# Cross-attention on the ring of eight PSUM banks, in text order on four engines, begun inside the self-attention's last steps, with routing behind its last tile

## The chip, the cores and the metric

One core of a Trainium2 chip runs the whole program in one launch. The metric is the device time of one execution in microseconds (us). The core has five engines with a queue of instructions each: PE (TensorE, matmuls and transposes through PE), DVE (VectorE), ACT (ScalarE), POOL (GpSimd) and SP, which here only issues DMAs. Each engine takes its instructions strictly in the order of its queue, and semaphores make one wait for another. PSUM has eight banks of 128 x 512 floats; PE writes there, and DVE or ACT copy from there to SBUF.

## The reference

A decoder layer on x of shape (2, 1024, 256), that is 2048 tokens in 16 tiles of 128, in fp32, cut to what matters here:

```python
x = x + attn(layernorm(x), ...)             # 16 heads, softmax + relative bias, then its own norm
x = x + xattn(layernorm(x), ctx, ctx, mask) # 16 heads of 16 against 77 context tokens
x = x + ffn(layernorm(x), ...)              # top-2 of 8 experts, plus a shared layer, then a norm

def xattn(query, key, value, mask, Wq, Wk, Wv, Wu, bu):
    scores = where(mask == 0, -1e9, q @ k.T)          # (b, h, 1024, 77)
    return softmax(scores) @ v  ->  heads side by side  @ Wu + bu

def ffn(x, ...):
    probs = softmax(flat @ gate_W)
    topk_w, topk_idx = top_k(probs, 2)                 # two experts per token
    out = 0.5 * gelu(flat @ shared_W + shared_b)
    for e in range(8):
        out += combine[:, e] * (gelu(flat @ W1[e] + b1[e]) @ W2[e] + b2[e])
    return norm(out)
```

## The kernel before, in words

**Self-attention (to about 549 us).** Two streams run over 128 steps of 8 per (batch, head group, half): stream A multiplies scores and takes row maxima on DVE (`mx`, L516); ten steps later (`LAG`) stream B multiplies shifted scores, ACT takes the exponent (`pt`, L560), PE multiplies by the values into one bank (`av`, L569), ACT copies that out (`part`, L581) and POOL adds it up (`avs`, L582). Once per eight steps `shift_queries` and `collect` run; every second half of the last head group, `collect` also normalizes and adds 512 tokens (a chunk c of four tiles) to the residual `xs` (`affine_residual`). Here all four engines run in the order of the text (`manual_schedule`), and every PSUM tile comes from one ring of eight banks, `one()`. Jobs that belong elsewhere are put into the table `between`, by step.

**Cross-attention and gate (549 to about 770 us).** Here only PE runs in text order; a scheduler orders DVE, ACT and POOL. PSUM is split into three tiles of two banks (`big`) and two of one. For each chunk `queries(c)` normalizes 512 tokens (statistics, `rstd` through a POOL pow L142, `xn` on DVE L163), transposes them, and projects. Then for each tile i of 128 tokens:

- scores: PE `sC` (L868), DVE adds the mask in two instructions of 616 (L875), DVE takes row maxima `cm` (L882), POOL subtracts (L883);
- ACT takes the exponent (L886);
- DVE sums rows `cs` (L888) and takes the reciprocal (L889), POOL multiplies (L890);
- `turn(i)`: 16 transposes on PE (`ppT`, L901), two copies on ACT (L902).

Per chunk `attend(c)` multiplies by the values (`pco`, L915) and by Wu (`pu`, L929) and adds to `xs` (L937); `gate(c)` normalizes again, writes `xn` to DRAM (`xnd`), and multiplies by the gate weights (`pg`, L949).

**Routing.** `choose(c)` finds the two best experts of each token in thirteen small DVE instructions (L741 to L759), `place(c)` counts the tokens ahead and builds one-hot rows and columns (L799, scaled on ACT, L807), `invert(c)` multiplies them into `places` (L817, L823). All three run chunk by chunk between the tiles. After chunk 3, a chain of small DVE instructions finds which expert owns each block of 256 slots and makes `to_row` and `from_row` (L1050, L1051): the addresses by which tokens are gathered. `shared(c)` multiplies by the shared layer's weights.

**Experts (to about 1100 us) and end.** 19 blocks of 256 slots: gather tokens (POOL's indirect DMA, L1107), transpose, two layers with Gelu between, scatter. While the first blocks are fetched, POOL takes a pow for the weights (L1075), adds a bias to `acc` and another to `xs` (eight instructions, L1187 and L190), and DVE finishes the weights (L1076 to L1078). Then results are loaded back, weighted, normalized and written.

## Time and profile before

| | us |
|---|---|
| median of 6 runs (1147.15 to 1152.01) | 1148.68 |
| profiled execution, its own time | 1149.66 |
| its span | 1147.9 |
| PE busy | 952.0 |
| DVE busy | 644.4 |
| ACT busy | 513.5 |
| POOL busy | 395.8 |

| stage of the profiled execution | from | to |
|---|---|---|
| self-attention's last `part` copy ends | | 548.85 |
| first / last POOL subtract of a tile (L883) starts | 583.00 | 715.09 |
| POOL multiply of the last tile (L890) ends | | 725.13 |
| logits of the last chunk (L741) | 765.01 | |
| `from_row` (L1051) | 781.25 | 781.44 |
| experts' first matmul (L1131) | 810.02 | |

The page gives busy time per engine, then 40 slices of the span in which a digit is tenths of busy time; PEclk is the clock granted to PE in tenths of full speed. In timelines a line has its start, its duration, engine, line of the kernel, operation, output<-inputs with shapes, and in brackets the idle time of that engine before it and what ended it. Instructions in a row of the same kind are merged (x8); a duration then runs from the first start to the last end. fp32 matmuls stand twice in the count.

### The profile page before, as it was taken

The numbers are of one execution on the slowest core, as the hardware profiler recorded it, in microseconds if no ns is written. First come the engines' busy times: TensorE is split into PE (matmuls) and PEld (weight loads), VectorE is DVE, ScalarE is ACT, GpSimd is POOL, SyncE is SP. The second block draws the span as 40 slices with busy tenths as digits, with TensorE's granted clock in tenths as the row PEclk, the third lists the DMA queues.
The fourth block names the chain that finished last, engine by engine and source line by source line (L and its number), as shares of the span: only waits on it lengthen the run. The fifth ranks groups of instructions, "written<-read, shape, count | busy, mean of one in ns | idle before, by whom it ended". The sixth has DMA issues, their size and how long they took to land. (4 is left out here: it accounts for less than half of the span.)

```text
span 1147.9 us, 15494 instructions
## 1 busy us (share of the span) xinstructions
PE 952.0 (83%) x5846; PEld 544.2 (47%) x5846; DVE 644.4 (56%) x1181; ACT 513.5 (45%) x969; POOL 395.8 (34%) x318
## 2 busy tenths in 40 slices
PE   4789999999797999999367786992799999999910
PEld 2443333333332333332134555671688888887810
DVE  5677558777876788884886688655300000000047
ACT  1328568677664678879034333321422222222201
POOL 2123223543322333334565535107323222222125
PEclk9989999999988999999689888776899999999965
DMA  8100000000000000000000000007255555554152
GB/s 166 32 1 1 1 2 1 1 1 1 1 1 1 1 2 1 1 1 1 15 0 2 18 1 19 19 19 252 64 188 194 188 176 167 175 179 158 46 165 73
DMA packets 59603, 67.07 MB, mean 58 GB/s; under 512 B 17947, under 2 KB 52408, under 8 KB 59520
## 3 DMA queue, kind: packets, MB, share of 16 engines
q1 hardware_dynamic: 44400, 53.10, 14.4%
q0 software_dynamic: 3648, 9.18, 2.3%
q10 hardware_dynamic: 11472, 3.70, 1.5%
q8 instruction: 49, 0.80, 0.3%
q14 instruction: 34, 0.28, 0.1%
HBM read 57.58 MB, written 9.18 MB: 58 GB/s over the span
## 5 line engine op out<-in xcount | busy, mean ns | idle before, releaser
L516 DVE TENSOR_REDUCE mx<-sA 128x1 f32<-128x512 f32 x512 | 317.7, 683 | 89.9 <-PE sB L552 74.9
L560 ACT ACTIVATE pt<-sB 128x512 f32<-128x512 f32 x512 | 266.3, 609 | 113.8 <-PE sB L552 113.2
L509 PE MATMUL sA<-kT,qc 32*128 32x512 f32 x1024 | 266.6, 637 | 0.0
L552 PE MATMUL sB<-qB,kT 32*128 32x512 f32 x1024 | 253.9, 626 | 10.4 <-DVE mx L516 10.4
L582 POOL TENSOR_TENSOR avs<-avs,part 128x512 f32<-128x512 f32 x112 | 143.0, 1276 | 306.2 <-ACT part L581 305.8
L1138 ACT ACTIVATE hT<-ph,b1s 128x256 f32<-128x256 f32 x152 | 72.0, 475 | 193.9 <-PE ph L1131 192.6
L1131 PE MATMUL ph<-xgT,w 128*128 128x256 f32 x608 | 138.5, 386 | 16.9 <-DVE xgT L1125 16.9
L1156 DVE TENSOR_TENSOR y<-po,b 128x512 f32<-128x512 f32 x19 | 13.1, 692 | 240.6 <-PE po L1149 240.6
L509 PEld LDWEIGHTS sA<-kT,qc 32*128 32x128 f32 x1024 | 102.7, 188 | 90.7 <-ACT pt L560 56.2
L1149 PE MATMUL po<-w,hT 128*128 128x256 f32 x608 | 138.8, 382 | 6.2 <-DVE y L1156 5.6
L569 PE MATMUL av<-pt,vaug 128*32 128x512 f32 x1024 | 141.1, 612 | 0.9 <-ACT pt L560 0.9
L1131 PEld LDWEIGHTS ph<-xgT,w 128*128 128x128 f32 x608 | 107.9, 192 | 44.6 <-DVE xgT L1125 17.7
L1149 PEld LDWEIGHTS po<-w,hT 128*128 128x128 f32 x608 | 114.2, 190 | 24.9 <-DVE y L1156 9.3
L552 PEld LDWEIGHTS sB<-qB,kT 32*128 32x128 f32 x1024 | 100.3, 187 | 51.6 <-issue 32.3
L1159 POOL DMA_INDIRECT pairs<-y,to_row x38 | 38.3, 1009 | 136.1 <-DMA pairs<-y,to_row 94.8
L1107 POOL DMA_INDIRECT xg<-xnd,from_row x38 | 37.2, 978 | 109.0 <-PE px L1121 76.6
L581 ACT COPY part<-av 128x512 f32<-128x512 f32 x112 | 68.8, 614 | 8.6 <-PE av L569 8.6
L569 PEld LDWEIGHTS av<-pt,vaug 128*32 128x32 f32 x1024 | 21.6, 109 | 101.8 <-DVE mx L516 84.6
L142 POOL TENSOR_TENSOR rstd<-rstd,nhalf 128x4 f32<-128x4 f32 x20 | 21.7, 1083 | 98.8 <-DVE rstd L141 98.4
L883 POOL TENSOR_TENSOR st<-st,cm 128x1232 f32<-128x1232 f32 x16 | 36.1, 2254 | 47.9 <-DVE cs L889 20.7
L901 PE MATMUL ppT<-ident,st 128*77 128x128 f32 x256 | 38.5, 311 | 15.3 <-POOL st L890 13.9
L902 ACT COPY PT<-ppT 77x1024 f32<-77x1024 f32 x32 | 31.2, 1007 | 36.0 <-PE ppT L901 36.0
(198 smaller groups left out, 989.2 us busy)
## 6 DMA issues: line engine op xcount, KB each, us to landing
w<-in_L_ffn_W_dram SPq DMA_DIRECT2D x38, 1024.0 KB, 5.9
b<-in_L_ffn_b_dram SPq DMA_DIRECT2D x19, 128.0 KB, 6.3
xs<-in_x_dram SPq DMA_DIRECT2D x4, 512.0 KB
xnd<-xn SPq DMA_DIRECT2D x4, 512.0 KB
w<-pairs ACTq DMA_DIRECT2D x4, 512.0 KB, 5.9
w<-pairs SPq DMA_DIRECT2D x4, 512.0 KB
out_dram<-acc SPq DMA_DIRECT2D x4, 512.0 KB, 2.8
mk<-in_mask_BxSxS_ik_dram SPq DMA_DIRECT2D x1, 616.0 KB
```

The costliest lines, as they stand in the source:

```text
L509: nc.tensor.matmul(s, lhsT=units[h // 4, "q"][r0 : r0 + 32, q0 : q0 + P], rhs=units[h // 4, "k", g % 2][r0 : r0 + 32, 512 * kh : 512 * kh ...
L516: nc.vector.tensor_reduce(largest[h][:, qt, hh : hh + 1, kh], s, AX.X, ALU.max)
L552: nc.tensor.matmul(s, lhsT=units[h // 4, "k", g % 2][r0 : r0 + 32, kt * P : (kt + 1) * P], rhs=shifted[h][r0 : r0 + 32, :], start=True, st ...
L560: nc.scalar.activation(powers[m, hh], s, AF.Exp, scale=1.0 / 16.0)
L569: nc.tensor.matmul(av[32 * hh : 32 * hh + 32, :], lhsT=vaug[:, kt, 4 * g + hh, :, b], rhs=powers.pop((m, hh)), start=True, stop=True,)
L581: nc.scalar.copy(part, av)
L582: nc.gpsimd.tensor_tensor(sums[h], sums[h], part, ALU.add)
L901: nc.tensor.transpose(pp[:T2, h, :], st[:, 8 * G + h, :], ident)
L1131: nc.tensor.matmul(ph[:, j, :], lhsT=w1[:, kc, hc * P : (hc + 1) * P], rhs=xgT[:, kc, :], start=(kc == 0), stop=(kc == 1),)
L1138: hidden[i] = nc.scalar.activation(hT[:, hc, :], ph[:, j, :], AF.Gelu, bias=b1s[:, i, hc : hc + 1])
L1149: nc.tensor.matmul(po[:, s, :], lhsT=hT[:, hc, s * P : (s + 1) * P], rhs=w2[:, hc, :], start=(hc == 0), stop=(hc == NH - 1),)
L1159: nc.gpsimd.indirect_dma_start(out=pairs[:, :], out_offset=bass.IndirectOffsetOnAxis(ap=to_row[:, k : k + 1], axis=0), in_=y[:, s, :], in_ ...
```

## The change

The diff does the following.

- **Banks.** The cross-attention, the gate and the routing use the same ring of eight single banks as the streams; the split into `big` and single tiles comes only behind routing. The mask is added in four DVE instructions of 308 per tile, `turn` copies four times 4 heads, a projection is two halves (`query(c, G)`), `shared(c)` two halves.
- **Order.** `manual_schedule` for four engines now reaches to the end of routing, so DVE, ACT and POOL also run in text order there.
- **Work moved between engines.** `xn` is made by ACT (`scale`, four activations with scale and offset); the offsets are a small DVE instruction (`offsets`). The one-hot rows are made and scaled in one DVE instruction each (`one_hots`), and ACT's scaling goes. Which engine copies a bank out is written at each call (`by_dve`, `by_act`).
- **Begun earlier.** `ask(0, 82)` and `ask(1, 103)` put statistics, scaling, transposes and projection of chunks 0 and 1 into steps 82 to 123 of the streams. `behind_step` puts the scores of tiles 0, 1 and 2 and the scaling of chunk 2 behind steps 129 to 138. In the last ten steps every third `part` copy goes to DVE.
- **Loop.** `front(i)`, `turn(i - 2)`, the jobs in `beside`, `mid(i - 1)` and `soft(i)` follow each other for tiles 3 to 16. The constants of routing (iotas) are made on POOL one per tile.
- **Routing.** `choose`, `count`, `place`, `one_hots` and `invert` run only behind the last tile, for tiles 0 to 7 together, then 8 to 11, then 12 to 15. The running count `earlier` is one reduction (`sum_up`) and further matmuls instead of one addition per tile.
- **Memory.** One SBUF tile `scrap` holds, one after another, the bias table, the weights and queries of the streams, the queries and scores of the cross-attention, and `acc`. `fsw` and `b1` are loaded by SP's queue instead of ACT's.

The core of the diff (lines that begin with a space are there before and after):

```diff
+    def offsets(c, live=None):
+        mv, r = moments.pop(c)[1], tokens[c]
         if live is not None:
             nc.vector.tensor_tensor(r[:, :4], r[:, :4], live, ALU.mult)
+        off = small.tile([P, 4], F32, tag="off", name=f"off{c}")
+        nc.vector.scalar_tensor_tensor(off, mv[:, :, 0], -1.0, r[:, :4], ALU.mult, ALU.mult)
+        tokens[c] = r, off, work.tile([P, 4, D], F32, tag="xn", name="xn")
+    def scale(c, ts=range(4)):
+        r, off, xn = tokens[c]
+        for t in ts:
+            nc.scalar.activation(
+                xn[:, t, :], xs[:, 4 * c + t, :], AF.Identity,
+                bias=off[:, t : t + 1], scale=r[:, t : t + 1],
+            )
...
-        nc.scalar.copy(part, av)
+        (by_act if m + LAG < steps + 2 or m % 3 else by_dve)(part, av)
...
+    def front(i):
+        c, t = i // 4, i % 4
+        b, st = c // 2, sts[i % 4]
+        off = mb[:, i, :].unsqueeze(1).to_broadcast([P, 4, T2])
+        for G in range(2):
+            for f in range(2):
+                s = one("sC")[:, : 4 * T2]
+                nc.tensor.matmul(s, ...)
+                h0 = 8 * G + 4 * f
+                nc.vector.tensor_tensor(
+                    st[:, h0 : h0 + 4, :], s.rearrange("p (j t) -> p j t", t=T2), off, ALU.add
+                )
+        cm = small.tile([P, H], F32, tag="cm", name="cm")
+        nc.vector.tensor_reduce(cm, st, AX.X, ALU.max)
+        nc.gpsimd.tensor_tensor(st, st, cm.unsqueeze(2).to_broadcast([P, H, T2]), ALU.subtract)
+    def soft(i):
+        nc.scalar.activation(sts[i % 4], sts[i % 4], AF.Exp)
+    def mid(i):
+        st = sts[i % 4]
+        cs = small.tile([P, H], F32, tag="cs", name="cs")
+        nc.vector.tensor_reduce(cs, st, AX.X, ALU.add)
+        nc.vector.reciprocal(cs, cs)
+        nc.gpsimd.tensor_tensor(st, st, cs.unsqueeze(2).to_broadcast([P, H, T2]), ALU.mult)
...
+    def ask(c, n):
+        jobs = {
+            0: lambda: measure(c, [0]),
+            1: lambda: measure(c, [1]),
+            4: lambda: measure(c, [2]),
+            5: lambda: measure(c, [3]),
+            8: lambda: deviation(c),
+            9: lambda: offsets(c, alive(c)),
+            10: lambda: scale(c, [0, 1]),
+            12: lambda: scale(c, [2, 3]),
+            14: lambda: turned(c, 0, by_act),
+            16: lambda: (turned(c, 1, by_dve), add_rows(c, bu)),
+            18: lambda: query(c, 0, by_act),
+            20: lambda: query(c, 1, by_dve),
+        }
+        for k, job in jobs.items():
+            between.setdefault(n + k, []).append(job)
+    ask(0, 82)
+    ask(1, 103)
+    behind_step = {
+        129: [lambda: front(0)],
+        131: [lambda: soft(0)],
+        132: [lambda: mid(0), lambda: front(1)],
+        134: [lambda: soft(1), lambda: measure(2), lambda: deviation(2)],
+        135: [lambda: mid(1), lambda: offsets(2, alive(2))],
+        138: [lambda: front(2), lambda: scale(2), lambda: soft(2)],
+    }
+    for n in range(steps + LAG + 1):
...
+        for job in behind_step.get(n, []):
+            job()
+    turned(2, 0, by_act)
+    turned(2, 1, by_act)
+    add_rows(2, bu)
+    collect(len(halves) - 1)
+    mid(2)
...
+    beside = {
+        3: [lambda: measure(3), lambda: deviation(3)],
+        4: [lambda: offsets(3, alive(3)), lambda: scale(3), lambda: query(2, 0, by_dve)],
+        5: [lambda: query(2, 1, by_dve), lambda: turned(3, 0, by_act),
+            lambda: turned(3, 1, by_dve), lambda: add_rows(3, bu)],
+        8: [lambda: query(3, 0, by_dve), lambda: query(3, 1, by_act)],
+        12: [lambda: shared(0)],
+    }
+    for c in range(3):
+        i = 4 * c + 6
+        ... attend(c, 0), attend(c, 1) at i; output(c, 0), output(c, 1) at i + 1
+        if c < 2:
+            ... measure(c), deviation(c) at i + 2
+            ... offsets(c), scale(c), keep_tokens(c), turned(c, 0, by_act),
+            ... turned(c, 1, by_dve), gate(c) at i + 3
+    turn(0)
+    for i in range(3, NT + 1):
+        if i < NT:
+            front(i)
+        turn(i - 2)
+        for job in beside.get(i, []):
+            job()
+        if i > 3:
+            mid(i - 1)
+        if i < NT:
+            soft(i)
+        if i > 5 and constants:
+            constants.pop(0)()
...
+    A, Z, C = (0, 8), (8, 12), (12, 16)
+    measure(2); deviation(2); shared(1); offsets(2); scale(2); keep_tokens(2)
+    choose(*A); turn(NT - 1); turned(2, 0, by_act); turned(2, 1, by_act); gate(2)
+    attend(3, 0); attend(3, 1); prk = count(*A); part = place(*A, prk)
+    hot0 = one_hots(0, 0, part)
+    output(3, 0); measure(3, (0, 1)); output(3, 1); measure(3, (2, 3)); deviation(3)
+    hot1 = one_hots(1, 4, part)
+    offsets(3); scale(3); keep_tokens(3); shared(2); invert(0, hot0); choose(*Z)
+    turned(3, 0, by_act); turned(3, 1, by_dve); gate(3)
+    sum_up(Z[0]); invert(1, hot1); prk = count(*Z); part = place(*Z, prk)
+    choose(*C); sum_up(C[0]); prk = count(*C); ...
+    hot2 = one_hots(2, 0, part); part = place(*C, prk); invert(2, hot2)
+    hot3 = one_hots(3, 0, part); invert(3, hot3)
```

The last block stands one call to a line in the file. `sts` has four score buffers, three in `scrap` and a fourth for tile 3, 7, 11 and 15; tile i uses `sts[i % 4]`.

## The prediction, made before the result was known

> **What bounds it now.** I read the page first, then the busy time by stage, then the timeline of the cross-attention stage engine by engine. The profiled execution took 1149.66 us (span 1147.9 and 1.8 around it), 0.98 above the median of 1148.68; I work out a difference and put it on the median.

> ```profile
> span 1147.9 us, 15494 instructions
> ...
> PE   4789999999797999999367786992799999999910
> DVE  5677558777876788884886688655300000000047
> ...
> PEclk9989999999988999999689888776899999999965
> ```

> Slices of 28.7 us. From slice 19 (550 us) to 27 no engine is near full and the TensorE clock falls to 6 to 8 tenths.

> ```profile
> core 0: us, PE busy (x) PEld busy (x) DVE busy (x) ACT busy (x) POOL busy (x), PEclk, DMA share, GB/s
> 82.00:540.00 458.00, 436.02 (x3359) 161.38 (x3362) 334.08 (x574) 326.43 (x640) 158.08 (x128) 0.98 0.00 1
> 575.00:600.00 25.00, 15.62 (x73) 9.73 (x74) 22.10 (x27) 8.17 (x8) 16.88 (x8) 0.86 0.00 0
> ...
> 680.00:720.00 40.00, 29.31 (x178) 22.20 (x180) 33.69 (x58) 16.79 (x22) 16.68 (x8) 0.84 0.04 14
> 720.00:750.00 30.00, 28.68 (x153) 18.75 (x146) 18.89 (x51) 8.52 (x16) 4.29 (x2) 0.73 0.06 19
> 750.00:770.00 20.00, 18.90 (x84) 16.25 (x84) 8.40 (x34) 4.80 (x11) 1.01 (x1) 0.76 0.08 26
> ...
> 782.00:810.00 28.00, 2.25 (x7) 1.15 (x7) 19.41 (x4) 0.00 (x0) 26.39 (x14) 0.50 0.65 228
> ```

> In the streams (82 to 540) PE is busy 95% at clock 0.98: it sets the pace. From 575 to 720, in the cross-attention's tiles, PE is at 62 to 78%, DVE at 78% (113.4 of 145) and POOL at 53% (77.3 of 145): none is full, and what counts is who waits for whom.

> ```profile
> 709.08 0.19 DVE L750 TENSOR_TENSOR cand<-cand,rank 128x32 f32<-128x32 f32 x1
> 715.21 2.17 DVE L750 TENSOR_TENSOR cand<-cand,rank 128x32 f32<-128x32 f32 x1
> 715.09 2.25 POOL L883 TENSOR_TENSOR st<-st,cm 128x1232 f32<-128x1232 f32 x1
> ...
> 713.00 1.92 PE L915 MATMUL pco<-PT,vx 77*32 77x512 f32 x16
> 718.11 0.41 PE L769 MATMUL prk<-taken,before 128*128 128x32 f32 x2 [3.18 <-DVE taken L759]
> 719.05 3.40 PE L915 MATMUL pco<-PT,vx 77*32 77x512 f32 x16
> ```

> Two things. The same DVE instruction (L750, two SBUF inputs) takes 0.19 us alone and 2.17 us while a POOL multiply of 2.25 us runs: it ends as that one ends. And a PE gap of 3.18 us is followed by sixteen `pco` matmuls in 3.40 us, which took 1.92 just before: half clock.

> ```profile
> 781.25 0.19 DVE L1051 TENSOR_SCALAR from_row<-to_row 128x46 int32<-128x46 int32 x1
> 790.48 18.38 DVE L1076 TENSOR_SCALAR wts<-wts 128x16 f32<-128x16 f32 x1 [8.96 <-POOL wts L1075]
> 799.61 9.22 POOL L190 TENSOR_TENSOR xs<-xs,beta_f 128x1024 f32<-128x1024 f32 x4
> 810.02 3.78 PE L1131 MATMUL ph<-xgT,w 128*128 128x256 f32 x8 [16.59 <-DVE xgT L1125]
> ```

> `from_row` (L1051) is the end of routing. Four gathers, a pow and eight adds on POOL follow; DVE's L1076 sits 18.38 us behind the adds and `xgT` behind it, so the experts' first matmul comes 28 us after `from_row`. The listing of the changed program has POOL and DVE in that order again, and weights and gathers land inside those 28 us. So everything from `from_row` on moves as one, and **the change is worth what it moves `from_row` (781.4)**.

> **Streams.** A step takes 2.93 us, DVE idling 0.44 to 0.55 and ACT 0.38 to 0.48 of it (columns before `mx` and `pt`). `ask` adds for two chunks: four `query` halves, of the shape of a `wq` projection, after which the next POOL add came 4.78 us later (391.56 to 396.34) against 2.93: +1.85 each, 7.4, less 0.83 that PE waits in the shift step where one falls; four `turned` halves, four transposes each (`po` L592, 0.59): 2.4; four pairs of `scale` on ACT (L1241, about 0.50 apart) over 0.4 of idle: 0.6 each, 2.4; `measure` (0.47 a step) in DVE's idle time: nothing, at most 0.5 a step or 4 if the cover is gone; `deviation` and `offsets`, three small DVE ops per chunk that can wait for a POOL add of 1.27: 1.0 in all, at most 7. Sum **+12.4**; bounds 5 (the PE work in gaps left by other waits) to 18.

> **Last steps and opening.** No trace shows these ops beside the B stream, so I walk the four queues with the stage's own durations. Front: sC 1.31, four adds of 308 for two of 616 (1.50 the pair; 1.6 is taken), `cm` 1.35, POOL 2.25. Soft: 1.23. Mid: `cs` 1.35 and 0.24, POOL 2.25. With the streams where they were, step 129 ends at 527.0: `cm`(0) 530.5, subtract 532.9, exp 534.4 behind step 131's copies, `cs` 536.1, multiply 540.5 behind one stream add; `cm`(1) 539.9, subtract 542.8, and ACT waits 1.0 for it. Collect(14) then holds DVE from 541 to 550.1, its POOL add queued behind that subtract and a stream add. The third of the `part` copies given to DVE (step 134) stands behind collect and leaves at 550.7; its bank is wanted near 548, so PE waits 3. The streams' last copy moves from 548.85 to 557.9. Then `cm`(2) 561.1, subtract 563.4, `add_rows` 565.8, collect(15) on DVE until 571.8 (its add is behind those two), `cs`(2) 573.4, `cm`(3) 576.4. Before, the subtract of tile 3 began at 600.77. With +12.4 it is at 588.9: **11.9 earlier**.

> **The loop, tiles 3 to 15.** A bare iteration is DVE's 4.6 (1.6+1.4+1.4+0.2); POOL needs 4.5, ACT 3.2, PE 3.2 (1.31, and 1.91 for `ppT`). Jobs cost in text order. Every fourth iteration has `attend` (32 `pco` rows, 3.64 at full clock) between `turn` and the next `front`: DVE then waits 3.3, and with two output adds that iteration is 12.4. The next has both `query` halves of chunk 3 (or `shared(0)`) and `measure`, DVE waiting for PE: 10.3. The next is the longest: `offsets` waits out the subtract (2.25), four `scale` 2.1, eight transposes 1.1, a copy 0.6, sixteen gate matmuls 1.95, and only then `cs`: 13.3. Sum 4.6+12.4+10.3+13.3 = 40.6 for four tiles. Walked from 576.4 the multiply of tile 15 ends at 696.9: 120.5 us, against 124.3 now (600.77 to 725.13): **3.8 less**, at full clock. Removed on the way: `xn` on DVE (0.33 each alone, 4.60 for two beside POOL at 695.35), routing's 0.2-us ops among POOL's, the 2.45 of `row` scalings on ACT per chunk.

> **The tail.** Now: tile 15's multiply 725.1, last output add 756.0, logits 765.0, `from_row` 781.4: 56.3. After: to the last output add 23.6 (routing of eight tiles stands in DVE's gaps), to logits 10.3 (one-hots of chunk 1, 2.9, come first), then 22.2 instead of 16.4, as chunk 2 is counted, placed and inverted after the last gate: count 3.1, place 1.6, choose 3.0, one-hots 2.8 (two `col` of half L799's size, 0.6 each, and eight rows of 128, taken at 0.19 between L141's 0.17 for 4 elements and L163's 0.33 for 256), place 1.6, 0.3, one-hots 2.8, invert 2.4, the eleven ops to `pick` 3.1, `ppk` and `from_row` 1.5. 56.1: **0.2 less**.

> **Clock.** Sum at full clock: −11.9−3.8−0.2 = −15.9. Between 575 and 782 the mean clock was 0.83, so a third of that time was at half. At half clock PE's terms grow: `ppT` 3.70 for 1.91, `pco` 7.0 for 3.64, `pg` 2.75 for 1.95, `sC` 2.42 for 1.31; along the walk 14 us per four tiles and 14 in the tail, 56 in all. Before, the cold stretches follow gaps of 3.2 to 6.0; the walk has a 6.9 (iteration 5) and a 4.7 (iteration 13), else gaps of 2.8 to 3.6. I take a third of the present share, 10%: +5.6. **−10.3: 1138.4.** Bounds: −15.9 at none, +3 at the present third.

> [...]

> SP's queue: `fsw`, `b1` and `fsb` move to it from ACT's ahead of the four `xnd` writes, which are not needed until `from_row`. No cost; if the last write were late, its landing (512 KB in about 3 us, the output's row) still fits into the 30 us between its `scale` and the gathers. The iotas on POOL (0.13 to 0.3 each) lie between its tiles: nothing while POOL has 0.1 to spare per tile, 3 at most.

> **Rivals.** (1) Slower: the clock. In text order no engine runs ahead of a stall, so every wait of DVE for PE is also a gap of PE, and if gaps near 3.3 drop the clock, PE's terms at half make the next gap. Point of decision: 28% of the stage at half clock; at the present 34% it is +3, at 50% +12 (1161). For it: 3.18 was enough. Against: most gaps are shorter than those now. (2) A larger gain: PE's inserted work sinks into the streams' waits (5 for 12.4) and DVE does not wait for PE in iterations 7 and 8 (3.3 and 3.0, three times): −10.3−7.4−16 = −34, 1115. For it: `ppT` of a tile may start earlier than walked, when POOL multiplies first. Against: POOL's order is text. (3) It nets out: some 40 hand-overs between engines at about 0.1, left out of the walk, and the routing chain eat the gain: within 2. (4) The 18-us wait of L1076 goes because POOL pauses between adds: −17 more; the order speaks against it.

> **Numbers.** Forecast 0.48, larger gain 0.20 with (4), nets out 0.08, slower 0.24. A measurement of this kernel tells 0.2% (2.3 us) from no change. Faster 0.68, same 0.08, slower 0.24. Range 1114 to 1156: the lower end is rival 2, the upper between +3 and +12; 1 in 10 left out at each end. Forecast's own range: 1129 to 1146.

> **Right or wrong.** Right if in the changed profile the streams' last `part` copy ends near 570, tile 3's subtract starts near 589 and tile 15's multiply ends near 710, with `from_row` near 771 and 28 us to the first expert matmul. Wrong if the streams end before 562 or after 578; if four tiles take under 36 or over 46 us; if the clock of 590 to 770 is under 0.85; or if the 28 us changes.

## The result: about 9 us slower

The changed kernel takes 1157.37 us (median of 20 runs, 1152.64 to 1165.10) against 1149.66 (46 runs of the kernel before, 1146.77 to 1152.41): a ratio of 1.0078, 95% interval 1.0066 to 1.0091. The ratio is taken over all runs and stands for 9 us; the two medians are 7.7 us apart. The profiled execution took 1155.64 us by its own time (span 1153.9), 1.7 under the median, so it shows 6 of the 9 us.

The page of the changed kernel:

```profile
span 1153.9 us, 15588 instructions
...
PE   4889999999797999999767777974699999999920
...
DVE  6677568778867787876676455356310000000037
...
PEclk9889999999898999999889776777799999999965
```

Slices are 28.8 us. From slice 22 (635 us) on the clock granted to PE reads 7 and 6, and in slices 22 to 25 DVE's digits are 4, 5, 5 and 3, where the kernel before has 6, 8, 8 and 6. The busy time by stage (columns as in the prediction) puts numbers on that:

```profile
82.00:540.00 458.00, 436.37 (x3323) 162.71 (x3326) 342.94 (x602) 321.49 (x631) 160.24 (x129) 0.98 0.00 1
575.00:600.00 25.00, 14.40 (x66) 10.51 (x67) 20.67 (x48) 12.27 (x23) 14.55 (x9) 0.83 0.06 18
...
680.00:720.00 40.00, 30.81 (x153) 20.24 (x150) 20.77 (x37) 15.72 (x26) 16.14 (x12) 0.71 0.04 14
720.00:750.00 30.00, 27.96 (x132) 19.84 (x131) 9.60 (x38) 8.70 (x17) 1.04 (x2) 0.70 0.05 18
750.00:770.00 20.00, 14.26 (x79) 12.86 (x77) 11.48 (x50) 3.50 (x7) 1.38 (x1) 0.80 0.07 26
...
782.00:810.00 28.00, 11.86 (x50) 10.00 (x49) 18.34 (x26) 1.17 (x2) 20.23 (x11) 0.69 0.71 250
```

The streams are as they were (0.98). From 680 to 720 the clock is 0.71 where it was 0.84, and DVE is busy for 20.8 of 40 us where it was 33.7. Part of that is routing, whose small operations now stand behind the loop; the rest is waiting. The prediction's markers, from the timelines of POOL, DVE and PE:

```profile
587.41 2.25 POOL L665 TENSOR_TENSOR st<-st,cm 128x1232 f32<-128x1232 f32 x1 [0.79 <-DVE cm L664]
...
717.78 2.25 POOL L676 TENSOR_TENSOR st<-st,cs 128x1232 f32<-128x1232 f32 x1
...
787.59 0.19 DVE L1175 TENSOR_SCALAR from_row<-to_row 128x46 int32<-128x46 int32 x1
...
796.82 18.38 DVE L1210 TENSOR_SCALAR wts<-wts 128x16 f32<-128x16 f32 x1 [4.10 <-POOL wts L1209]
...
816.35 3.78 PE L1265 MATMUL ph<-xgT,w 128*128 128x256 f32 x8 [16.72 <-DVE xgT L1259]
```

| us | before | predicted | after |
|---|---|---|---|
| streams' last `part` copy ends | 548.85 | 570 | 568.43 |
| tile 3's subtract starts | 600.77 | 588.9 | 587.41 |
| tile 15's multiply ends | 725.13 | 710 | 720.03 |
| `from_row` starts | 781.25 | 771 | 787.59 |
| experts' first matmul | 810.02 | 799 | 816.35 |
| loop, second row to third | 124.4 | 120.5 at full clock | 132.6 |
| tail, third row to fourth | 56.1 | 56.1 at full clock | 67.6 |

The opening won 13.4 us, a little more than forecast. The loop lost 8.2 against before and the tail 11.5. The 28.8 us behind `from_row`, with the 18.38 us of the weights' first operation, are the same to a hundredth. So all of the miss lies between tile 3's subtract and `from_row`, and there the timeline of PE shows this:

```profile
609.00 3.32 PE L686 MATMUL ppT<-ident,scrap 128*77 128x128 f32 x16 [3.57 <-POOL scrap L676]
612.25 3.64 PE L697 MATMUL pco<-PT,vx 77*32 77x512 f32 x32
...
627.29 1.97 PE L686 MATMUL ppT<-ident,scrap 128*77 128x128 f32 x16 [3.57 <-POOL scrap L676]
...
671.54 3.70 PE L686 MATMUL ppT<-ident,scrap 128*77 128x128 f32 x16 [3.57 <-POOL scrap L676]
...
694.62 3.69 PE L686 MATMUL ppT<-ident,scrap 128*77 128x128 f32 x16 [1.95 <-POOL scrap L676]
698.25 7.06 PE L697 MATMUL pco<-PT,vx 77*32 77x512 f32 x32
705.23 2.35 PE L652 MATMUL sC<-kbd,scrap 64*128 64x308 f32 x8
...
732.48 7.06 PE L697 MATMUL pco<-PT,vx 77*32 77x512 f32 x32
...
742.90 6.38 PE L711 MATMUL pu<-cwu,oT 128*128 128x256 f32 x16
```

Three of the `ppT` rows stand behind the same gap of 3.57 us: sixteen transposes took 3.32, 1.97 and 3.70 us. The clock fell at two of the three. From 686.75 to 707.5 and from 731.25 to 748.5 it stayed down although PE was busy for 18.4 of 20.5 and for 17.1 of 17.1 us: `pco` took 7.06 us there both times where full clock gives 3.64 (612.25), `pu` 6.38 where it gives 3.62 (663.11). And this comes back through DVE, whose next tile stands behind PE (timeline of DVE):

```profile
706.73 1.74 DVE L660 TENSOR_TENSOR st<-sC,mb 128x308 f32<-128x308 f32 x4 [9.97 <-PE sC L652]
```

### The profile page after: what moved, and what is told of

Its sections match the earlier page's. It is cut to its first block, busy times and chain, and to the rows that moved or that the text cites. A ratio compares the mean times of both kernels' runs of the same rounds, so it can differ in the third digit from the quotient of the medians.

```text
span 1153.9 us, 15588 instructions
## 1 busy us (share of the span) xinstructions
PE 970.9 (84%) x5874; PEld 562.5 (49%) x5874; DVE 619.4 (54%) x1197; ACT 520.4 (45%) x1008; POOL 394.2 (34%) x317
## 5 line engine op out<-in xcount | busy, mean ns | idle before, releaser
L520 PE MATMUL sA<-kT,scrap 32*128 32x512 f32 x1024 | 266.7, 639 | 0.0
L563 PE MATMUL sB<-qB,kT 32*128 32x512 f32 x1024 | 256.5, 629 | 10.4 <-DVE mx L527 10.4
L520 PEld LDWEIGHTS sA<-kT,scrap 32*128 32x128 f32 x1024 | 103.3, 189 | 90.1 <-ACT pt L571 51.3
L1241 POOL DMA_INDIRECT xg<-xnd,from_row x38 | 37.3, 982 | 117.8 <-PE px L1255 73.8
L592 ACT COPY part<-av 128x512 f32<-128x512 f32 x110 | 67.0, 609 | 14.4 <-PE av L580 14.4
L687 ACT COPY PT<-ppT 77x512 f32<-77x512 f32 x64 | 34.2, 587 | 49.2 <-PE ppT L686 48.8
L686 PE MATMUL ppT<-ident,scrap 128*77 128x128 f32 x192 | 33.2, 344 | 25.2 <-POOL scrap L676 25.2
L686 PEld LDWEIGHTS ppT<-ident,scrap 128*77 128x77 f32 x192 | 30.1, 196 | 31.3 <-POOL scrap L676 29.3
```

The source lines that it names most:

```text
L520: nc.tensor.matmul(s, lhsT=units[h // 4, "q"][r0 : r0 + 32, q0 : q0 + P], rhs=units[h // 4, "k", g % 2][r0 : r0 + 32, 512 * kh : 512 * kh ...
L563: nc.tensor.matmul(s, lhsT=units[h // 4, "k", g % 2][r0 : r0 + 32, kt * P : (kt + 1) * P], rhs=shifted[h][r0 : r0 + 32, :], start=True, st ...
L592: (by_act if m + LAG < steps + 2 or m % 3 else by_dve)(part, av)
L686: nc.tensor.transpose(pp[:T2, h, :], st[:, 4 * k + h, :], ident)
```

## Experiments

Each time stands against runs of the kernel before on the same chip. Kernels that fill PE's gaps share one helper: a matmul that nobody reads, written to the bank that the real work will use, ahead of it in PE's queue.

```diff
+    def fill(bank, n):
+        for _ in range(n):
+            nc.tensor.matmul(bank[:, :D], lhsT=ident, rhs=cwu[:, 0, :], start=True, stop=True)
```

All kernels on the changed text, from their profiles ("clock" is the mean granted clock of 575 to 785 us; loop and tail as in the table above):

| kernel | clock | loop | tail | ratio to before | 95% |
|---|---|---|---|---|---|
| changed kernel | 0.77 | 132.6 | 67.6 | 1.0078 | 1.0066 to 1.0091 |
| e8_fill_tiny | 0.72 | 140.4 | 70.0 | 1.0105 | 1.0083 to 1.0126 |
| e12_gates_only | 0.74 | 142.7 | 74.4 | 1.0106 | 1.0079 to 1.0132 |
| e9_part_act | 0.72 | 140.1 | 69.8 | 1.0128 | 1.0107 to 1.0150 |
| e4_ask1_late | 0.72 | 149.9 | 69.8 | 1.0183 | 1.0165 to 1.0202 |
| e3_late_weigh | 0.76 | 132.6 | 70.6 | 0.9942 | 0.9919 to 0.9964 |
| e13_waits_only | 0.85 | 118.4 | 67.8 | 0.9915 | 0.9896 to 0.9934 |
| e1_fill | 0.87 | 118.4 | 62.3 | 0.9870 | 0.9843 to 0.9898 |
| e7_fill_gates | 0.94 | 118.2 | 59.0 | 0.9850 | 0.9832 to 0.9869 |
| e10_fill_gates_late | 0.94 | 118.2 | 65.0 | 0.9713 | 0.9695 to 0.9730 |
| e14_fill_weigh_text | 0.94 | 118.5 | 57.9 | 0.9694 | 0.9674 to 0.9714 |

**e1_fill: is it the clock?**

```diff
-        turn(i - 2)
+        turn(i - 2, FILLS.get(i, 0))     # {4: 6, 5: 6, 6: 5, 8: 5, 9: 6, 10: 3, 12: 5, 14: 3, 16: 6}
...
-            pp = one("ppT")...
+            pp = one("ppT")
+            if k == 0:
+                fill(pp, n)
...
-    gate(2)
+    gate(2, 3)                           # and 1 to 6 at the other small waits of gates and routing
```

> The changed kernel with idle stretches of PE filled: matmuls of 128x128 by 128x256 that nobody reads are written to a bank just ahead of the real work that PE waits to do there (2.3 us ahead of ppT in seven iterations of the loop, 0.5 to 2.7 us at twelve smaller waits of gates and routing). Nothing else moves. Theory CLOCK (the loop and the tail lost to the half clock what the walk at full clock had won): the mean clock of 575 to 785 rises from 0.78 to over 0.92, tile 3's subtract stays near 587, tile 15's multiply ends near 708 to 712 instead of 720.0 and from_row comes near 764 to 772 instead of 787.6; time to before 0.987 to 0.995 instead of 1.0078. Rival WALK (the walk at full clock was too short: waits between engines, not PE's speed, set the loop): the clock rises all the same, but tile 15's multiply still ends within 3 us of 720 and from_row within 4 us of 787.6; time to before 1.004 to 1.011. Rival COST (the filling itself stands in the way of the real work): slower than 1.010.

Measured: 1135.48 us, ratio 0.9870, that is 22 us under the changed kernel, with 70 matmuls of 0.45 us more in PE's queue (in nine iterations of the loop, not the seven that were expected). Its stage 575 to 785, and the second `attend` of its loop:

```profile
575.00:785.00 210.00, 183.19 (x990) 136.27 (x988) 129.00 (x306) 70.02 (x119) 88.88 (x64) 0.87 0.11 39
```

```profile
684.87 2.03 PE L694 MATMUL ppT<-ident,scrap 128*77 128x128 f32 x16
686.83 3.64 PE L705 MATMUL pco<-PT,vx 77*32 77x512 f32 x32
690.40 1.31 PE L657 MATMUL sC<-kbd,scrap 64*128 64x308 f32 x8
```

`ppT`, `pco` and `sC` have their full-clock times, 2.03, 3.64 and 1.31 us. The loop takes 118.4 us where the walk at full clock had said 120.5. CLOCK holds, WALK and COST fall. (The clock reached 0.87 only, not the 0.92 that was expected: the tail still spends 25 of its 62 us at half clock.)

**e8_fill_tiny: the clock, or merely a busy queue?**

```diff
-        for _ in range(n):
-            nc.tensor.matmul(bank[:, :D], lhsT=ident, rhs=cwu[:, 0, :], start=True, stop=True)
+        for _ in range(2 * n):
+            nc.tensor.matmul(bank[:, :E], lhsT=ident, rhs=fgw[:, 0, :], start=True, stop=True)
```

> As e1_fill, at the same places and for about the same PE time, but each filling matmul (128x128 by 128x256, 0.45 us) is replaced by two of the gate's shape (128x128 by 128x8, 0.24 us each in the gate's rows). Theory WORK (the clock follows the work in the array, not whether PE has an instruction; what e1_fill gained came from the clock): the clock of 575 to 785 stays at 0.70 to 0.80, tile 15's multiply ends at 717 to 724, the time is that of the changed kernel or up to 5 us over it, ratio to before 1.005 to 1.013. Rival BUSY (any instruction in the gap keeps the clock up): like e1_fill, clock near 0.88, ratio 0.984 to 0.991. Rival OTHER (the filling helps otherwise than by the clock, for example because PE wakes faster behind a busy queue): clock under 0.80, but ratio under 1.000.

Measured: 1162.14 us, ratio 1.0105. The same stage:

```profile
575.00:785.00 210.00, 194.56 (x1030) 154.78 (x1030) 109.51 (x264) 68.07 (x111) 71.95 (x53) 0.72 0.04 13
```

PE is busier than in any other kernel here, 194.6 of 210 us, and its clock is no higher than without the filling, 0.72 against 0.77. So PE's busy time was no sign of its clock here (e1 has 183.2 us at 0.87): matmuls of 128 x 8 in the gaps did not hold it up. BUSY and OTHER fall: a queue that was merely busy did not win the time that e1 won.

**e12_gates_only and e13_waits_only: which gaps?** e12 has `fill(bank[:, D:], 1)` ahead of each token tile in `gate`, e13 has the `FILLS` of e1 and nothing else.

> The changed kernel with filling matmuls only inside the four gates (one of 0.45 us ahead of each token tile, 1.8 us per gate), none at the waits for POOL. Theory GATES (the three longest cold stretches, 17 to 21 us each, begin in a gate, and pco behind it does not end them): the cold time of 575 to 785 falls from 104 to 45 to 75 us, from_row comes at 770 to 780, ratio 0.994 to 1.002. Rival WAITS (the waits for POOL's multiplication start the half clock, and the gates only continue it): cold time over 80 us, ratio 1.004 to 1.012.

> The changed kernel with filling matmuls only ahead of ppT in nine iterations of the loop (1.4 to 2.7 us each), none in gates or behind the loop. Theory GATES: the short cold stretches (3.5 to 7 us, at 584, 598, 608, 670 and 717) go, the long ones stay: cold time 65 to 85 us, tile 15's multiply ends at 708 to 714, from_row at 774 to 781, ratio 0.996 to 1.003. Rival WAITS: cold time under 60 us, ratio under 0.994.

Measured: e12 1161.84 us, ratio 1.0106, and 116 us at half clock from 540 to 785, where the changed kernel has 102 (the expectation's 104 counts from 540 too; the profile of e12 is of one of its two slowest runs, 1168.06 of 1159.05 to 1168.14); e13 1140.63 us, ratio 0.9915, loop 118.4. The theory GATES falls for the loop: filling the waits for POOL alone brings the whole loop to full clock but for 16 us, and filling the gates alone brings nothing. In the time at half clock e13 is nearer to GATES (72 us from 540 on, where WAITS had under 60), because the tail keeps all of its own: 37 us, as in the changed kernel. I had read the beginnings of the cold stretches in e1, where the long gaps were filled already, as if they were those of the changed kernel.

**e7_fill_gates: both.** e1 with e12's filling in the gates.

> e1_fill with one more filling matmul (0.45 us) ahead of each of the four token tiles in the gate (1.8 us more for each of four gates), since in e1_fill every long cold stretch but one begins 1 to 2 us after the first gate matmul of 128x8, with PE hardly idle. Theory WORK (the 128x8 matmuls count as idle time for the clock): the stretches that begin at 640.7, 678.2 and 715.7 go, pco behind gate(2) takes 3.64 instead of 7.06 and pu 3.62 instead of 6.71, and the tail from tile 15's multiply to from_row falls from 62.4 to 54 to 58 us; 3 to 8 us faster than e1_fill, ratio 0.980 to 0.985. Rival COST (PE sets the pace there, and the 7 us of filling are paid in full): as fast as e1_fill or up to 6 us slower, ratio 0.987 to 0.993.

Measured: 1133.67 us, ratio 0.9850, 0.2% under e1 with intervals that overlap. The clock is 0.94, and in the tail `pco` and `pu` are back at full speed (timeline of PE):

```profile
718.75 3.64 PE L705 MATMUL pco<-PT,vx 77*32 77x512 f32 x32
...
724.13 3.70 PE L719 MATMUL pu<-cwu,oT 128*128 128x256 f32 x16
```

The tail falls to 59.0 us, 3.3 under e1 and 1 over what WORK had said; 2.0 of it reach `from_row` (764.5 against 766.5), since tile 3's subtract came 1.6 later in the profile of e7. From that subtract to `from_row` e7 spends 7 of 177 us at half clock, and the walk at full clock had said 120.5 + 56.1 = 176.6.

**e6_fill_before: does the kernel before gain as much?** The same helper in the kernel before, ahead of the transposes, `pu` and `prk` that wait longest there.

> The kernel before with idle stretches of PE filled in the same manner (9 us ahead of the first transposes, 1.8 to 2.7 us ahead of four of the ppT, 2.3 us ahead of the first pu, 1.8 us ahead of two prk, 0.9 us ahead of each other pxT). Theory CLOCK: the clock of 575 to 781 rises from 0.83 to over 0.92, and, PE's time being on the path in a third to a half of the 72 us that were at half clock, the kernel gains 6 to 16 us: ratio 0.986 to 0.995. Rival SCHEDULE (the scheduler's order hides PE's slow stretches behind DVE and POOL): within 0.3% of before, whatever the clock.

Measured: 1148.10 us, ratio 0.9988 (0.9976 to 1.0000). The clock rises from 0.83 to 0.89, the time at half clock between 575 and 785 falls from 72 to 46 us, and `from_row` stays at 781.4 (781.25 before). By the whole time SCHEDULE holds: 26 us less of half clock gained nothing clear there, and 31 us less (e13) were worth 17 us in the changed kernel. But the stages of e6 show both a gain and a loss. Its tail takes 53.2 us instead of 56.1, with 10 us at half clock instead of 22, and the last tile's multiply ends 3.1 us later than before (728.26 against 725.13). The scheduler also put DVE's, ACT's and POOL's instructions into another order than before. What made the part ahead of the tail longer, the filling, the other order or something else, e6 cannot tell apart.

**e4_ask1_late: was it right to begin in the streams?**

```diff
-    ask(1, 103)
...
     beside = {
-        3: [lambda: measure(3), lambda: deviation(3)],
+        3: [lambda: measure(1), lambda: deviation(1), lambda: offsets(1, alive(1)),
+            lambda: scale(1), lambda: turned(1, 0, by_act), lambda: turned(1, 1, by_dve),
+            lambda: add_rows(1, bu), lambda: query(1, 0, by_dve), lambda: query(1, 1, by_act),
+            lambda: measure(3), lambda: deviation(3)],
```

> The changed kernel with the statistics, scaling, transposes and projection of chunk 1 taken out of the streams' steps 103 to 123 and put in front of tile 4's scores. Theory INSERT (the step of the prediction: 6.2 us per chunk in the streams, where PE has no room): the streams end 5 to 7 us earlier than 567.9, but the same work, now a chain across DVE, POOL, ACT and PE with nothing else ready, costs 8 to 13 us ahead of tile 4; 2 to 7 us slower than the changed kernel, time to before 1.010 to 1.014. Rival SUNK (the work was hidden in the streams' waits): the streams end under 3 us earlier, and the whole is 8 us or more slower, ratio over 1.014. Rival WASTE (it is dearer in the streams than outside): as fast as the changed kernel or faster, ratio under 1.008.

Measured: 1169.36 us, ratio 1.0183, 12 us slower than the changed kernel. From the first `pt` to the last the streams take 483.7 us instead of 488.0, so chunk 1 costs them 4.3 us, not the 6.2 that INSERT had; from tile 3's subtract to tile 7's it is 46.9 instead of 32.6 us. None of the three theories has both numbers: the work is dearer outside, by 14 us, and cheaper inside than priced. (A part of the 14 us may be the clock: the loop has 78 us at half clock, the changed kernel's 58.) For chunk 1, beginning in the streams was the good part of the change.

**e9_part_act: the wait behind `collect`.** `by_act(part, av)` in all steps.

> The changed kernel with all part copies on ACT again (none on DVE in the last ten steps). The prediction priced the DVE copy behind collect(14) at a PE wait of 3 us; the trace shows 4.81 us, with a cold stretch of 7 us behind it. Theory STALL: the wait at 556 to 561 goes, the streams end 2 to 5 us earlier than 567.9, and the whole is 1 to 5 us faster than the changed kernel, ratio 1.003 to 1.007. Rival QUEUE (something else of DVE's, collect and its normalization, holds the next step: the qB or sB banks, or ACT has become the bound): the streams end within 1 us, ratio 1.006 to 1.010. Rival WORSE (ACT was late without the help): slower, ratio over 1.010.

PE's wait in the changed kernel, and the same `av` in e9 (timelines of PE):

```profile
560.89 1.93 PE L580 MATMUL av<-pt,vaug 128*32 128x512 f32 x8 [4.81 <-DVE part L592]
```

```profile
554.65 1.47 PE L580 MATMUL av<-pt,vaug 128*32 128x512 f32 x8
```

The wait of 4.81 us is gone, and from the first `part` copy to the last the streams take 477 us instead of 479. But tile 3's subtract comes as long after the first `part` copy as before (498.4 us in both): DVE's chain of `collect`, `cs` and `offsets` sets it (in e9 DVE is busy without a gap from 553.2 to 569.7). And the whole is slower, 1165.01 us, ratio 1.0128, by a loop of 140.1 us with the same instructions in the same order as in the changed kernel (132.6). WORSE has the ratio but not its reason: ACT was not late; the clock was 0.72 instead of 0.77. The section on hardware shows where the two loops part.

**e3_late_weigh and e11_before_late: the 18 us of the weights' first operation.**

```diff
         with tc.issue_after(sorted_at.ins), tc.issue_after(fetched[1].ins):
-            weigh()
             for c in range(4):
...
         with tc.issue_after(hidden[1].ins):
+            weigh()
             for c in range(4):
                 finish_shared(c)
```

> The changed kernel with weigh() (a subtraction, a pow and three small DVE operations) issued behind the first Gelu of block 1 instead of ahead of the eight POOL additions. Theory PORT (L1210 is held 18.38 us by the eight additions on POOL, and xgT, which reads PSUM, only stands behind it in DVE's queue): xgT runs as soon as px is there, the experts' first matmul comes 12 us after from_row instead of 28.8, and the whole is 14 to 17 us shorter: time to before 0.993 to 0.996. Rival DMA (weights and gathers land late, and end the wait anyway): under 5 us shorter, first matmul still over 23 us after from_row, ratio over 1.003. Rival LATER (the same operations, now inside the experts, or the late gathers of block 2, hold the experts up by as much): first matmul early, but the time within 4 us of the changed kernel's.

> The kernel before with weigh() taken from ahead of the eight POOL additions (as in e3_late_weigh). The scheduler of that kernel puts the five operations among those of choose(3), in front of the gathers. Theory PORT: L1076 no longer waits 18.38 us for the additions, the experts' first matmul comes 12 to 14 us after from_row instead of 28.8, at a cost of up to 3 us in routing: time to before 0.985 to 0.990, so the 18 us were there for the taking before and after alike and explain nothing of the change's loss. Rival DMA: under 5 us faster (ratio over 0.9955), because there the weights land later after from_row than in the changed kernel.

Measured: e3 1141.13 us, 0.9942; e11 1132.70 us, ratio 0.9852 (0.9836 to 0.9869). The scheduler did not put `weigh` behind the Gelu in either kernel, but ahead, between the operations of `choose` and ahead of POOL's additions. In e3 the operation takes 0.17 us there instead of 18.38, and the experts' first matmul comes 12.6 us after `from_row` in e3 and 11.6 in e11. PORT holds in both. Most of the 28 us that the prediction had left standing could be had in either kernel and have no part in the difference between them.

**e10_fill_gates_late and e14_fill_weigh_text: a kernel that beats both.** e10 is e7 and e3 together; e14 gives `weigh` a place in the text.

```diff
     choose(*C)
+    wts = rt.tile([P, 2, NT], F32, name="wts")
+    w0, w1 = wts[:, 0, :], wts[:, 1, :]
+    nc.vector.tensor_tensor(w1, tops[:, 1, :], tops[:, 0, :], ALU.subtract)
+    nc.gpsimd.tensor_tensor(w1, euler, w1, ALU.pow)
     sum_up(C[0])
...
     part = place(*C, prk)
+    nc.vector.tensor_scalar(w0, w1, 1.0, None, ALU.add)
+    nc.vector.reciprocal(w0, w0)
+    nc.vector.tensor_tensor(w1, w1, w0, ALU.mult)
```

> e7_fill_gates and e3_late_weigh together: PE's gaps filled, weigh() behind the first Gelu of block 1. If the two gains add, ratio to before = that of e7_fill_gates less 0.0136 (e3_late_weigh stood at 0.9942, the changed kernel at 1.0078): 0.966 to 0.974. If the weights' DMA becomes the bound, because from_row comes 20 us earlier and the weights of the first blocks do not, the sum falls short by up to 10 us: 0.974 to 0.983.

> e10_fill_gates_late with weigh() at a place of its own in the text: in the trace of e10 the scheduler had put it between the operations of choose, where DVE waited 2.96 us for POOL's pow (2.90) ahead of the last count. Here the subtraction and the pow stand behind choose of tiles 12 to 15 and the three small operations 6 us later, so that nothing waits for the pow. If that wait was on the path: 2 to 5 us faster than e10, ratio 0.967 to 0.970; if the experts' weights end the wait by now: within 1 us of e10, 0.970 to 0.972.

Measured: e10 1118.39 us, ratio 0.9713: the gains add (0.9850 less 0.0136). e14 1112.96 us, ratio 0.9694 (0.9674 to 0.9714), 3.1% under the kernel before; the step from e10 to e14 lies within the intervals, so neither of its two theories is decided, though its tail is 7 us shorter. In e14 the experts' first matmul follows `from_row` (760.7) by 13.3 us (timeline of PE):

```profile
773.98 1.99 PE L1281 MATMUL ph<-xgT,w 128*128 128x256 f32 x8 [0.40 <-DVE xgT L1275]
```

## Why the prediction was wrong

**The clock: the step that failed.** The forecast took 10% of the stage at half clock, "a third of the present share", because most gaps of the walk were shorter than those of the kernel before. From tile 3's subtract to `from_row` the changed kernel spent 94 of 200 us at half clock, 47%, and its clock of 590 to 770 was 0.77, under the 0.85 that the prediction had named as a sign of being wrong. The prediction's own price, 56 us for all of it, makes that 26 instead of 5.6: −15.9 + 26 = +10, and the runs say +9. They measure the price too: from the changed kernel to e7 half clock falls by 87 us (94 less 7) and loop and tail together by 23.0 (200.2 to 177.2), 0.26 us for each, against 0.24 in the prediction (56 over 176.6 + 56). That is a mean, not a rate that holds everywhere: the loop of e13 has 16 us at half clock, that of e7 has 2, and they take 118.4 and 118.2 us.

The fault was in the argument, not only in a size. I judged gaps by their length. The rows show one length, 3.57 us, with both outcomes, and stretches of 17 to 21 us at half clock that no gap explains. The kernel before could have told me: I had read its cold stretches (those at half clock) as following gaps of 3.2 to 6.0 us, but four of the eleven between tile 3's subtract and `from_row` begin during the gate's matmuls or within 1 us of their end, behind gaps of 1.1 to 1.3 us. One of them begins at 709.1 (timeline of PE, before):

```profile
706.36 1.95 PE L949 MATMUL pg<-fgw,xnT 128*128 128x8 f32 x16 [1.10 <-ACT xnT L92]
...
709.78 3.29 PE L901 MATMUL ppT<-ident,st 128*77 128x128 f32 x16
```

And the walk's gaps were computed at full clock: with the clock down, `pco` holds `sC` back, DVE waits 9.97 us for it, POOL waits for DVE, and the next `ppT` waits for POOL. Rival 1 had described that loop and its point of decision (28%); it was given 24% and its upper end, +12 at half of the stage, was cut from the range.

**What held.** The opening: tile 3's subtract at 587.4 for 588.9. Within it the terms were off against each other: chunk 1 costs the streams 4.3 us, not 6.2. The wait behind the DVE `part` copy was 4.81, not 3, and e9 shows that it cost the opening nothing. The loop at full clock: 118.2 to 118.5 us in five kernels for 120.5. The tail at nearly full clock: 59.0 (e7) and 57.9 (e14) for 56.1. The 28 us behind `from_row`: 28.76 for 28.77. The sum at full clock was −15.9; e7, which is the changed kernel at nearly that clock, has −16.8 in the same three stages (−13.5, −6.2, +2.9) and 17 us by its ratio.

**The other rivals.** The larger gain (2) needed PE's work to sink into the streams' waits for 5 us in all; one chunk alone cost 4.3. It also needed a loop shorter by 16 us, which no kernel has (its own two waits, 3.3 and 3.0 us three times, make 19). Netting out (3), by hand-overs that the walk leaves out, is not seen at full clock: e7 keeps the 16.8 us. The wait of the weights' operation (4) stayed, as forecast, because the order stayed. (The POOL row that the prediction sets beside the 2.17 us of L750 is a subtract, not a multiply; the reading is the same.)

**What the kernel before loses to the clock** stays open. Its clock was 0.83, not much better than 0.77. e6 raised it and gained 2.9 us in the tail, 0.25 us for each of the 12 us at half clock that went, but nothing clear in the whole. If a better clock is worth less there, a likely reason, argued and not shown, is the order: there a scheduler places DVE's, ACT's and POOL's instructions, so that an engine has other work when PE is late. In text order on four engines each stands at its own next line until PE, at half speed, has delivered. A walk at full clock cannot show what that slack was worth.

## What to carry to other kernels

When a stage leaves PE gaps like those ahead of `ppT` here (1.95 to 5.77 us), price its PE terms at both clocks before anything else, and do not decide by gap length, since 3.57 us had both outcomes: the share of half clock came out of the loop (47%), where the forecast had put one in (10%). Where the gaps cannot be closed, fill them with matmuls of the size used here (128 x 128 by 128 x 256) into a bank that is about to be used; in text order this was worth 22 us here; in the scheduled kernel before, where it also changed the order of other engines, nothing clear. Before blaming a long wait on the engine that it names, look at what runs on POOL for exactly that long: here five tiny operations, put ahead of POOL's additions, were worth 16 us.

## What the runs showed of the hardware that I had not expected

Four kernels run the same instructions in the same order from tile 3's subtract to tile 7's, at different places on the grid. In each, `ppT` starts 21.5 to 21.6 us after the subtract, behind the gap of 3.57 us, and an edge lies just before it, at which the clock falls. In the changed kernel and e3 the edge is 0.62 and 0.65 us ahead of `ppT`, and the clock is back at the next one; `pco` takes 3.64 us and the four tiles 32.6 and 32.5. In e12 and e9 it is 0.69 and 0.85 us ahead, and the clock stays down; `pco` takes 7.06 us and the four tiles 37.1 and 37.0. The rows of e12 (timeline of PE), against those at 609.00 and 612.25 above:

```profile
604.54 3.70 PE L686 MATMUL ppT<-ident,scrap 128*77 128x128 f32 x16 [3.57 <-POOL scrap L676]
608.17 7.06 PE L697 MATMUL pco<-PT,vx 77*32 77x512 f32 x32
```

So a shift of less than a tenth of a microsecond goes with about 4.5 us in four tiles. These are four traces read afterwards; no run moved the loop on its own. The run-to-run spread of the changed kernel fits (1152.6 to 1165.1 us, against 1146.8 to 1152.4 before): its five slowest runs, 1161.7 us and more, have a mean clock of 0.899 or 0.900, all others 0.904 to 0.911.

**Not every matmul brought the clock back.** `pco` (77 rows by 32 columns, four side by side) ran for 7.06 us at half clock twice in the changed kernel and once in e1, without a rise before it ended, while `pu` (128 x 128) was followed by full clock 5.4 us after its start in the changed kernel and 6.1 in e1. e8 shows the other side for 128 x 8 (clock 0.72 with 194.6 of 210 us busy). Counted over the kernel before and the changed kernel (560 to 790 us): five steps of the grid at half clock that `pco` filled to nine tenths or more were followed by half clock again, and twelve that one of `ppT`, `pq`, `pu`, `psh` or `pin` filled as far were followed by full clock, all of them. Whether size in rows, in columns or the number of elements counts was not tried.
